# A gated expert layer and feed-forward block: every engine's order of instructions written in the kernel

## Chip, core and metric

The kernel runs on one core of one Trainium2 chip. The metric is the device time of one execution in microseconds (us), as the median of several runs.

## What is computed

There are 2048 tokens with 512 features in float32. A token id chooses one of four experts; the expert's one 512 x 512 matrix serves as gate, up and down projection. The result goes back onto the token, gated by a tanh. Then a layer norm and a feed-forward block follow; its outputs, weighted by the two best of eight routing scores, are summed into the first eight rows of the output.

```
hs = layernorm(x)
g = silu(hs @ M[e].T); u = hs @ M[e].T          # M = ctx_2048, e = expert of the token
x = x + tanh(g_xattn) * ((g * u) @ M[e].T)
xr = layernorm(x)
p = softmax(xr @ wr.T); top 2 of 8 -> gates (normed), indices
h = silu(silu(xr @ w1.T) @ w3.T) @ w2.T
out = zeros; out[indices[:, k]] += gates[:, k] * h   (k = 0, 1)
x = x + tanh(g_ffn) * out
```

## The kernel before

**Passes.** The tokens are sorted by expert into 17 passes of 128 places. Passes 0 to 12 (`NF` = 13) hold one expert each. Passes 13 to 16 are split in four groups of 32 places, each group with its own expert, and so need four matrices. The preamble works out the sorting on VectorE (DVE) with a few small products on TensorE (PE): `from_row` (where the tokens of a pass lie), `to_row` (where they go) and `which` (which expert's matrix a place needs). `which0` is the first pass's entry of that table, worked out ahead of the rest.

**One pass** runs through these steps:
- `gather`: an indirect DMA from POOL's queue brings the pass's rows into one of five buffers x. `load` issues on SP one DMA of 1 MB for a one-expert pass and four for a split pass, into eight buffers m; the row address comes from `which` through a register.
- `prepare`: DVE takes the moments of x and subtracts the mean (`h_a`); PE transposes h_a in four pieces (`tp_a`); ScalarE (ACT) copies the result out of PSUM (`hT`); DVE works out the inverse root of the variance in nine small operations on one column (`rs_a`).
- `up`: PE multiplies by the expert's matrix (`z`), ACT takes a sigmoid with `rs_a` as scale, and DVE multiplies twice (`g`).
- `turn`: PE transposes g (`tp_g`) and ACT copies it (`gT`).
- `down`: PE multiplies again (`y`), DVE adds it onto x, POOL scatters x to the output, and DVE norms the new x (`st_f`, `rs_f`, `h_f`).
- `place_out`: PE transposes h_f (`tp_f`), and ACT copies it into a block's `hT2`. A split pass takes four copies, each to a column read from a table.

**Feed-forward.** Four passes' worth of tokens (512) make a block; there are four blocks. `ffn` is a generator that is advanced by `step()`: four pieces of `u` (w1) with sigmoid and product, one piece for the routing scores (`lg`) and `route`, and four pieces of `v` (w3). At a block's end `acc` adds the four pieces with the gates; the last block takes its last two in turned form (`accT`). After the last block w2 is applied once to the eight sums.

**Order.** The main loop runs over 17 passes and two more iterations. Iteration i issues up(i), place_out(i-2), a step, down(i-1), turn(i), the gather and loads of pass i+3, a step and prepare(i+2). The program text is not the order in which an engine runs it: the tile framework's scheduler orders each engine's instructions itself, by priority and by what it expects to be ready. A few `issue_after` blocks hold instructions behind a named one. The order of passes is a list in the kernel.

```
order = [0, 1, 2, 3, 4, NF, 5, 6, NF + 1, 7, 8, 9, NF + 2, 10, 11, 12, NF + 3]
```

PSUM has four buffers for z, y, u and v (`ps_mm`), three for transposes and lg (`ps_tp`) and one for the sums.

Of the kernel before, what the change touches and what calls it, by code (L numbers as in the profile page):

```python
# [8 lines left out]
F32 = mybir.dt.float32  # L9
# [15 lines left out]
def tile_gated_moe_ffn(  # L25
# [234 lines left out]

    start = ct_([P, 2 * E - 1], F32, "start")
    nc.vector.scalar_tensor_tensor(start, cut[:, 1 : 2 * E], 0.0, steps, ALU.is_le, ALU.mult)
    which0 = ct_([P, 1], I32, "which0")
    with nc.allow_low_precision("whole numbers below 4096"):
        nc.vector.tensor_reduce(which0, start, AX.X, ALU.add)
    from_row = ct_([P, NP], I32, "from_row")
    known = nc.vector.tensor_scalar(from_row, tok, -1.0, 0.0, ALU.add, ALU.max)

    which = ct_([P, NU], I32, "which")
    first = ct_([P, NU - NF], I32, "first")  # L270
    to_row = ct_([P, NP], I32, "to_row")

    later = ct_([P, 2 * E, NU], F32, "later")

    def matrix_table():

        nc.vector.tensor_tensor(
            later,
            place0.unsqueeze(1).to_broadcast([P, 2 * E, NU]),
            cut[:, 1 : 2 * E + 1].unsqueeze(2).to_broadcast([P, 2 * E, NU]),  # L280
            ALU.is_ge,
        )
        stepped = ct_([P, 2 * E - 1, NU], F32, "stepped")
        nc.vector.tensor_tensor(
            stepped,
            later[:, 0 : 2 * E - 1],
            steps.unsqueeze(2).to_broadcast([P, 2 * E - 1, NU]),
            ALU.mult,
        )
        with nc.allow_low_precision("whole numbers below 4096"):  # L290
            nc.vector.tensor_reduce(which, stepped.rearrange("p e n -> p n e"), AX.X, ALU.add)

# [27 lines left out]
    nc.gpsimd.memset(aT, 0.0)  # L320

    def moments(xt, name):
        st = small.tile([P, 6], F32, tag="st", name=f"st_{name}")
        nc.vector.bn_stats(st, xt)  # L324
        mv = small.tile([P, 2], F32, tag="mv", name=f"mv_{name}")
        nc.vector.bn_aggr(mv, st)
        return mv

    def inverse_root(mv, name):


        v = small.tile([P, 1], F32, tag="v", name=f"v_{name}")
        nc.vector.tensor_scalar_add(v, mv[:, 1:2], EPS)  # L333
        r = small.tile([P, 1], F32, tag="r", name=f"r_{name}")
        nc.vector.tensor_scalar(
            r.bitcast(I32), v.bitcast(I32), -0.5, float(0x5F3759DF), ALU.mult, ALU.add
        )
        q = small.tile([P, 1], F32, tag="q", name=f"q_{name}")
        nc.vector.scalar_tensor_tensor(q, r, v, r, ALU.mult, ALU.mult)
        w = small.tile([P, 1], F32, tag="w", name=f"w_{name}")  # L340
        nc.vector.tensor_scalar(w, q, 0.375, -1.25, ALU.mult, ALU.add)
        nc.vector.tensor_scalar(w, w, q, 1.875, ALU.mult, ALU.add)
        nc.vector.tensor_mul(r, r, w)
        nc.vector.scalar_tensor_tensor(q, r, v, r, ALU.mult, ALU.mult)
        nc.vector.tensor_scalar(q, q, -0.5, 1.5, ALU.mult, ALU.add)
        rs = small.tile([P, 1], F32, tag="rs", name=f"rs_{name}")
        nc.vector.tensor_mul(rs, r, q)
        return rs
# [7 lines left out]

    order = [0, 1, 2, 3, 4, NF, 5, 6, NF + 1, 7, 8, 9, NF + 2, 10, 11, 12, NF + 3]
    assert sorted(order) == list(range(NP))
    xs, rss, hTs, gTs, gs, hs2, mats = {}, {}, {}, {}, {}, {}, {}

# [9 lines left out]

    def prepare(p):

        mv = moments(xs[p], f"a{p}")
        h = work.tile([P, D], F32, tag="h", name=f"h_a{p}")
        centred = nc.vector.tensor_scalar(h, xs[p], mv[:, 0:1], None, ALU.subtract)
        tp = transposed(h, f"a{p}")
        hT = work.tile([P, KC * P], F32, tag="hT", name=f"hT_{p}")
        parts = 2 if p == order[0] else 1
        n = KC * P // parts
        for i in range(parts):  # L380
            nc.scalar.copy(hT[:, i * n : (i + 1) * n], tp[:, i * n : (i + 1) * n])  # L381
        hTs[p] = hT
        rss[p] = inverse_root(mv, f"a{p}")
        return centred

    def load(p):
# [3 lines left out]
        for i in range(n0, n0 + n):  # L390
            at = nc.values_load(
                which0[0:1, :] if p == order[0] else which[0:1, i : i + 1],
                engines=[SP],
                min_val=0,
                max_val=(E - 1) * D,
                skip_runtime_bounds_check_because="an expert's number, times D",
            )
            m = mp.tile([P, KC, D], F32, tag="m", name=f"m_{i}")
            dma = nc.sync.dma_start(
                m, ctxT[bass.ds(at, D), :].rearrange("(k p) f -> p k f", p=P)  # L400
            )
            mats[p].append(m)
        return dma

# [22 lines left out]

    def turn(p):
        tp = transposed(gs.pop(p), f"g{p}")
# [4 lines left out]
    def down(p):  # L434
# [12 lines left out]
        )  # L447
        mv = moments(xt, f"f{p}")
        rs = inverse_root(mv, f"f{p}")
        h = work.tile([P, D], F32, tag="h", name=f"h_f{p}")  # L450
        nc.vector.tensor_scalar(h, xt, mv[:, 0:1], rs, ALU.subtract, ALU.mult)  # L451
        hs2[p] = h

    def place_out(p):

# [66 lines left out]
    def ffn(b):  # L522
# [30 lines left out]
        def gated(t):  # L553
# [10 lines left out]
            nc.scalar.activation(s2, v, AF.Sigmoid)  # L564
            return s2, nc.vector.tensor_mul(s2, s2, v)  # L565

# [21 lines left out]
        for t in range(TT):  # L588
            s2, done = gated(t)
            s2s.append(s2)  # L590
            if t < TT - 1:
                yield
            if b == NB - 1 and t == TT - 2:
                for i in range(TT - 2):
                    add(i, s2s[i])
                a = work.tile([P, D], F32, tag="a", bufs=1, name="a")
                nc.scalar.copy(a, acc)
        if b < NB - 1:
            for t in range(TT):
                add(t, s2s[t])  # L600
        else:
            add_turned(TT - 2, s2s[TT - 2])
            tp = transposed(a, "sum")
            with tc.issue_after(done.ins):
                nc.vector.tensor_reduce(
                    aT[:, :, 0:NR],
                    tp.rearrange("p (k t q) -> p k q t", k=KC, t=TT)[:, :, 0:NR, :],
                    AX.X,
                    ALU.add,
                )  # L610
            add_turned(TT - 1, s2s[TT - 1])
        yield


    block_of = [min(p // TT, NB - 1) for p in order]
    ready = {}
    for b in range(NB):
        ready.setdefault(max(i for i in range(NP) if block_of[i] == b), []).append(b)
    AHEAD = 3
    load(order[0])  # L620
    for p in order[:AHEAD]:
        gather(p)
    with tc.issue_after(known.ins):
        matrix_table()
        for p in order[1:AHEAD]:
            load(p)
    centred = prepare(order[0])
    with tc.issue_after(centred.ins):
        prepare(order[1])
        row_tables()  # L630
    running = []

    def step():
        if running and next(running[0], 0) == 0:
            running.pop(0)

    for i in range(NP + 2):
        if i < NP:
            up(order[i])
        if i >= 2:  # L640
            place_out(order[i - 2])
            running += [ffn(b) for b in ready.get(i - 2, [])]
        step()
        if 1 <= i <= NP:
            down(order[i - 1])
        if i < NP:
            turn(order[i])
        if i + AHEAD < NP:
            gather(order[i + AHEAD])
            loaded = load(order[i + AHEAD])  # L650
            with tc.issue_after(loaded.ins):
                if i == 0:
                    w1 = load_w(w1T, "w1")
                    wr = load_w(wrT, "wr")
                if order[i + AHEAD] == NF:
                    w3 = load_w(w3T, "w3")
                    w2 = load_w(w2T, "w2")
        step()
        if i + 2 < NP:
            prepare(order[i + 2])  # L660
    while running:
        step()

    x_first = ct_([P, P], F32, "x_first")
    nc.vector.memset(x_first, 0.0)
    for k in range(KC):
# [55 lines left out]
```

## Time and profile before

| | |
|---|---|
| median of 3 runs | 304.76 us (304.38 to 304.84) |
| profiled execution, its own time | 305.67 us |
| its span in the profile | 303.9 us |
| PE busy | 278.0 us, 91% |
| DVE busy | 153.9 us, 51% |
| ACT busy | 65.6 us, 22% |
| POOL busy | 38.3 us, 13% |
| bytes moved by DMA | 42.54 MB, mean 140 GB/s |

Busy times are unions over an engine's instructions. A float32 matmul appears as two records of 0.592 us each that overlap, so a record's length is not its price; the distance from start to start is. A name such as `z<-m,hT` gives the tile that an instruction writes and those it reads. What ended an idle time is inferred from semaphores. The span is what the profiler saw; the profiled execution's own time has 1.8 us around it.

### The profile page before, as it was taken

The numbers are of one execution on the slowest core, as the hardware profiler recorded it, in microseconds if no ns is written. First come the engines' busy times: TensorE is split into PE (matmuls) and PEld (weight loads), VectorE is DVE, ScalarE is ACT, GpSimd is POOL, SyncE is SP. The second block draws the span as 40 slices with busy tenths as digits, with TensorE's granted clock in tenths as the row PEclk, the third lists the DMA queues.
The fourth block names the chain that finished last, engine by engine and source line by source line (L and its number), as shares of the span: only waits on it lengthen the run. The fifth ranks groups of instructions, "written<-read, shape, count | busy, mean of one in ns | idle before, by whom it ended". The sixth has DMA issues, their size and how long they took to land.

```text
span 303.9 us, 3486 instructions
## 1 busy us (share of the span) xinstructions
PE 278.0 (91%) x1150; PEld 126.4 (42%) x1150; DVE 153.9 (51%) x610; ACT 65.6 (22%) x125; POOL 38.3 (13%) x60
## 2 busy tenths in 40 slices
PE   0169999979999999999799999999989999999994
PEld 0134455524435434535343444445334444344433
DVE  5445477772636954618816276646262455201511
ACT  1012232231312231303302222323021212102120
POOL 5410111311200211101212011100010010000000
PEclk9999999999999999999999999999999999999999
DMA  0799997551509931509925141910000000000000
GB/s 1 230 398 365 409 377 302 208 207 44 179 29 352 345 128 27 181 2 333 405 84 175 36 173 47 372 64 35 0 37 0 35 11 3 0 0 1 2 0 2
DMA packets 20722, 42.54 MB, mean 140 GB/s; under 512 B 2143, under 2 KB 2207, under 8 KB 20704
## 3 DMA queue, kind: packets, MB, share of 16 engines
q1 hardware_dynamic: 17664, 33.66, 30.8%
q0 software_dynamic: 2720, 8.65, 7.8%
q8 instruction: 9, 0.15, 0.2%
q14 instruction: 9, 0.07, 0.1%
q10 hardware_dynamic: 320, 0.01, 0.1%
HBM read 38.10 MB, written 4.47 MB: 140 GB/s over the span
## 4 chain that ended last, share of the span: by engine, by line
PE 85%; DVE 6%; DMA 2%; issue 2%; POOL 2%; ACT 1%; POOLq 0%; ACTq 0%
PE y L410 20%; PE u L529 19%; PE v L556 18%; PE z L410 17%; DMA x<-in_x_dram,from_row 2%; PE tp_a L354 2%; PE tp_f L354 2%; PE tp_g L354 2%; PE acc L568 2%; PE lg L544 1%; DVE x L439 1%; DVE st_f L324 1%; POOL lane L141 1%; DVE st_a L324 1%; DVE h_f L451 0%
## 5 line engine op out<-in xcount | busy, mean ns | idle before, releaser
L410 PE MATMUL z<-m,hT 128*32 128x512 f32 (+1 forms) x232 | 68.0, 612 | 0.5 <-ACT hT L381 0.5
L410 PE MATMUL y<-m,gT 128*32 128x512 f32 (+1 forms) x232 | 64.0, 595 | 0.4 <-ACT gT L431 0.4
L529 PE MATMUL u<-hT,w 128*128 128x512 f32 x128 | 57.9, 597 | 1.5 <-ACT hT L461 1.5
L556 PE MATMUL v<-w,s 128*128 128x512 f32 x128 | 57.2, 595 | 0.0
L410 PEld LDWEIGHTS y<-m,gT 128*32 128x32 f32 (+1 forms) x232 | 23.7, 146 | 33.2 <-issue 31.2
L410 PEld LDWEIGHTS z<-m,hT 128*32 128x32 f32 (+1 forms) x232 | 23.9, 151 | 30.6 <-issue 29.2
L529 PEld LDWEIGHTS u<-hT,w 128*128 128x128 f32 x128 | 23.2, 190 | 28.6 <-issue 25.6
L556 PEld LDWEIGHTS v<-w,s 128*128 128x128 f32 x128 | 23.4, 190 | 26.6 <-issue 25.4
L440 POOL DMA_INDIRECT out_dram<-x,to_row x17 | 17.0, 997 | 116.7 <-DVE x L439 115.8
L439 DVE SCALAR_TENSOR_TENSOR x<-y,tg,x 128x512 f32<-128x512 f32 x17 | 12.8, 751 | 36.0 <-PE y L410 36.0
L538 DVE TENSOR_TENSOR s<-sg,u 128x512 f32<-128x512 f32 x16 | 11.0, 685 | 35.0 <-ACT sg L537 34.9
L424 DVE SCALAR_TENSOR_TENSOR g<-z,rs_a,g 128x512 f32<-128x512 f32 x17 | 12.7, 748 | 29.4 <-ACT g L423 29.4
L363 POOL DMA_INDIRECT x<-in_x_dram,from_row x17 | 16.6, 976 | 72.4 <-issue 27.5
L565 DVE TENSOR_TENSOR s<-s,v 128x512 f32<-128x512 f32 x16 | 11.0, 685 | 27.4 <-ACT s L564 27.4
L537 ACT ACTIVATE sg<-u 128x512 f32<-128x512 f32 x16 | 9.6, 597 | 53.4 <-PE u L529 44.0
L354 PE MATMUL tp_a<-ident,h_a 128*128 128x128 f32 x68 | 11.4, 294 | 10.2 <-DVE v_a L333 5.8
L423 ACT ACTIVATE g<-z,rs_a 128x512 f32<-128x512 f32 x17 | 11.7, 687 | 37.2 <-PE z L410 25.7
L431 ACT COPY gT<-tp_g 128x512 f32<-128x512 f32 x17 | 10.0, 585 | 45.0 <-PE tp_g L354 45.0
L564 ACT ACTIVATE s<-v 128x512 f32<-128x512 f32 x16 | 9.6, 597 | 39.9 <-PE v L556 39.9
L381 ACT COPY hT<-tp_a 128x512 f32<-128x512 f32 (+1 forms) x18 | 10.0, 563 | 37.4 <-PE tp_a L354 37.4
L354 PEld LDWEIGHTS tp_a<-ident,h_a 128*128 128x128 f32 x68 | 8.5, 149 | 20.8 <-issue 15.9
L324 DVE BATCH_NORM_STATS2 st_a<-x 128x6 f32<-128x512 f32 x17 | 11.6, 679 | 6.4 <-DMA x<-in_x_dram,from_row 6.4
(133 smaller groups left out, 209.1 us busy)
## 6 DMA issues: line engine op xcount, KB each, us to landing
m<-in_ctxT_dram SPq DMA_DIRECT2D x29, 1024.0 KB
w<-in_w1T_dram SPq DMA_DIRECT2D x1, 1024.0 KB
w<-in_w3T_dram SPq DMA_DIRECT2D x1, 1024.0 KB
w<-in_w2T_dram SPq DMA_DIRECT2D x1, 1024.0 KB
x<-in_x_dram,from_row POOLq DMA_INDIRECT x17, 4.9
out_dram<-x,to_row POOLq DMA_INDIRECT x17, 4.9
wr<-in_wrT_dram SPq DMA_DIRECT2D x1, 64.0 KB
x_first<-out_dram SPq DMA_DIRECT2D x4, 4.0 KB
```

Of the source, the lines that this page charges most:

```text
L324: nc.vector.bn_stats(st, xt)
L354: nc.tensor.transpose(tp[:, k * P : (k + 1) * P], h[:, k * P : (k + 1) * P], ident)
L363: nc.gpsimd.indirect_dma_start(out=xt, out_offset=None, in_=x, in_offset=bass.IndirectOffsetOnAxis(ap=from_row[:, p : p + 1], axis=0),)
L410: nc.tensor.matmul(out_ps[i * n : (i + 1) * n, :], lhs[:, k * P + i * n : k * P + (i + 1) * n], m[:, k, :], start=(k == 0), stop=(k == KC ...
L423: nc.scalar.activation(g, z, AF.Sigmoid, scale=rs)
L424: nc.vector.scalar_tensor_tensor(g, z, rs, g, ALU.mult, ALU.mult)
L439: nc.vector.scalar_tensor_tensor(xt, y, tg[:, 0:1], xt, ALU.mult, ALU.add)
L440: nc.gpsimd.indirect_dma_start(out=out, out_offset=bass.IndirectOffsetOnAxis(ap=to_row[:, p : p + 1], axis=0), in_=xt, in_offset=None, bou ...
L529: nc.tensor.matmul(u, w1[:, k, m * P : (m + 1) * P], hT[:, k, 0:TB], start=(k == 0), stop=(k == KC - 1),)
L538: nc.vector.tensor_mul(s1[:, m, :], sg, u)
L556: nc.tensor.matmul(v, s1[:, k, t * P : (t + 1) * P], w3[:, k, :], start=(k == 0), stop=(k == KC - 1),)
L565: return s2, nc.vector.tensor_mul(s2, s2, v)
```

## The change

The kernel is traced under `tc.manual_schedule()`: every engine runs its instructions in the order of the program text. The `issue_after` blocks go. The text is arranged anew:

- Each iteration issues up(i), gather and loads of pass i+3, down(i-1), turn_out(i-2), norms, a step, turn_mid(i), turn_in(i+1), a step. `prepare` is cut in two: the norm (`centre` and `scale` ahead of the loop, `norms` in it) and the transposes with their copy (`turn_in`, one pass ahead).
- `norms` works out the second norm of pass i-1 and the first of pass i+2 together; `inverse_roots` alternates the operations of both.
- The first passes are written out ahead of the loop.
- `matrix_table` is called for the first two places ahead of `from_row` and for the rest later; `which0` goes.
- The order of passes changes: split passes come later. The norms' h tiles have four buffers instead of three.
- At a block's end, `acc` is issued with the next step's work (`SHORT`).
- `x_first` is cleared early on POOL, not late in the text on DVE.

The core of the diff:

```diff
-    start = ct_([P, 2 * E - 1], F32, "start")
-    nc.vector.scalar_tensor_tensor(start, cut[:, 1 : 2 * E], 0.0, steps, ALU.is_le, ALU.mult)
-    which0 = ct_([P, 1], I32, "which0")
-    with nc.allow_low_precision("whole numbers below 4096"):
-        nc.vector.tensor_reduce(which0, start, AX.X, ALU.add)
+    def matrix_table(n0, n1):
+        n = n1 - n0
...
+    matrix_table(0, 2)
     from_row = ct_([P, NP], I32, "from_row")
-    known = nc.vector.tensor_scalar(from_row, tok, -1.0, 0.0, ALU.add, ALU.max)
+    nc.vector.tensor_scalar(from_row, tok, -1.0, 0.0, ALU.add, ALU.max)
...
+    x_first = ct_([P, P], F32, "x_first")
+    nc.gpsimd.memset(x_first, 0.0)
...
-    def inverse_root(mv, name):
+    def inverse_roots(mvs_, names):
+        n = range(len(names))
...
+        for i in n:
+            nc.vector.tensor_scalar_add(v[i], mvs_[i][:, 1:2], EPS)
+        for i in n:
+            nc.vector.tensor_scalar(
+                r[i].bitcast(I32), v[i].bitcast(I32), -0.5, float(0x5F3759DF), ALU.mult, ALU.add
+            )
...
-    order = [0, 1, 2, 3, 4, NF, 5, 6, NF + 1, 7, 8, 9, NF + 2, 10, 11, 12, NF + 3]
+    order = [0, 1, 2, 3, 4, 5, 6, NF, 7, 8, NF + 1, 9, 10, NF + 2, 11, 12, NF + 3]
...
+    def centre(p):
+        mvs[p] = moments(xs[p], f"a{p}")
+        hs[p] = work.tile([P, D], F32, tag="h", bufs=4, name=f"h_a{p}")
+        nc.vector.tensor_scalar(hs[p], xs[p], mvs[p][:, 0:1], None, ALU.subtract)
+    def scale(*ps):
+        for p, rs in zip(ps, inverse_roots([mvs.pop(p) for p in ps], [f"a{p}" for p in ps])):
+            rss[p] = rs
+    def turn_in(p):
+        tp = transposed(hs.pop(p), f"a{p}")
...
+    def norms(p_in, p_out):
+        names, mv = [], []
+        if p_out is not None:
+            xt = x1s.pop(p_out)
+            mv.append(moments(xt, f"f{p_out}"))
+            names.append(f"f{p_out}")
+        if p_in is not None:
+            mv.append(moments(xs[p_in], f"a{p_in}"))
+            names.append(f"a{p_in}")
+        rs = inverse_roots(mv, names)
...
         if b < NB - 1:
             for t in range(TT):
                 add(t, s2s[t])
+            yield SHORT
...
+    def step():
+        if running:
+            r = next(running[0], 0)
+            if r == 0:
+                running.pop(0)
+            if r in (0, SHORT):
+                step()
     load(order[0])
+    load(order[1])
+    for i in range(5):
+        gather(order[i])
+    centre(order[0])
+    turn_in(order[0])
+    centre(order[1])
+    scale(order[0], order[1])
+    matrix_table(2, NU)
+    load(order[2])
+    w1 = load_w(w1T, "w1")
+    wr = load_w(wrT, "wr")
+    load(order[3])
+    row_tables()
+    centre(order[2])
+    scale(order[2])
+    up(order[0])
+    turn_in(order[1])
+    up(order[1])
+    turn_mid(order[0])
+    turn_in(order[2])
+    down(order[0])
+    turn_mid(order[1])
+    norms(order[3], order[0])
+    load(order[4])
+    w3 = load_w(w3T, "w3")
+    w2 = load_w(w2T, "w2")
-    for i in range(NP + 2):
+    for i in range(2, NP + 2):
         if i < NP:
             up(order[i])
-        if i >= 2:
-            place_out(order[i - 2])
-            running += [ffn(b) for b in ready.get(i - 2, [])]
+        if i + 3 < NP:
+            gather(order[i + 3])
+            load(order[i + 3])
+        if i <= NP:
+            down(order[i - 1])
+        else:
+            step()
+        turn_out(order[i - 2])
+        if i <= NP:
+            norms(order[i + 2] if i + 2 < NP else None, order[i - 1])
         step()
-        if 1 <= i <= NP:
-            down(order[i - 1])
+        running += [ffn(b) for b in range(NB) if last[b] == i - 2]
         if i < NP:
-            turn(order[i])
...
+            turn_mid(order[i])
+        if i + 1 < NP:
+            turn_in(order[i + 1])
         step()
-        if i + 2 < NP:
-            prepare(order[i + 2])
     while running:
         step()
...
-    with tile.TileContext(nc) as tc:
+    with tile.TileContext(nc) as tc, tc.manual_schedule():
         tile_gated_moe_ffn(tc, *args)
```

More of the change, by code (lines that the diff above doesn't have):

```diff
@@ L259, in tile_gated_moe_ffn @@
         )
-    start = ct_([P, 2 * E - 1], F32, "start")
-    nc.vector.scalar_tensor_tensor(start, cut[:, 1 : 2 * E], 0.0, steps, ALU.is_le, ALU.mult)
-    which0 = ct_([P, 1], I32, "which0")
-    with nc.allow_low_precision("whole numbers below 4096"):
-        nc.vector.tensor_reduce(which0, start, AX.X, ALU.add)
-    from_row = ct_([P, NP], I32, "from_row")
-    known = nc.vector.tensor_scalar(from_row, tok, -1.0, 0.0, ALU.add, ALU.max)
     which = ct_([P, NU], I32, "which")
-    first = ct_([P, NU - NF], I32, "first")
-    to_row = ct_([P, NP], I32, "to_row")
     later = ct_([P, 2 * E, NU], F32, "later")
-    def matrix_table():
+    stepped = ct_([P, 2 * E - 1, NU], F32, "stepped")
+    def matrix_table(n0, n1):
+        n = n1 - n0
         nc.vector.tensor_tensor(
-            later,
-            place0.unsqueeze(1).to_broadcast([P, 2 * E, NU]),
-            cut[:, 1 : 2 * E + 1].unsqueeze(2).to_broadcast([P, 2 * E, NU]),
+            later[:, :, n0:n1],
+            place0[:, n0:n1].unsqueeze(1).to_broadcast([P, 2 * E, n]),
+            cut[:, 1 : 2 * E + 1].unsqueeze(2).to_broadcast([P, 2 * E, n]),
             ALU.is_ge,
         )
-        stepped = ct_([P, 2 * E - 1, NU], F32, "stepped")
         nc.vector.tensor_tensor(
-            stepped,
-            later[:, 0 : 2 * E - 1],
-            steps.unsqueeze(2).to_broadcast([P, 2 * E - 1, NU]),
+            stepped[:, :, n0:n1],
+            later[:, 0 : 2 * E - 1, n0:n1],
+            steps.unsqueeze(2).to_broadcast([P, 2 * E - 1, n]),
             ALU.mult,
@@ L290, in matrix_table @@
         with nc.allow_low_precision("whole numbers below 4096"):
-            nc.vector.tensor_reduce(which, stepped.rearrange("p e n -> p n e"), AX.X, ALU.add)
+            nc.vector.tensor_reduce(
+                which[:, n0:n1], stepped[:, :, n0:n1].rearrange("p e n -> p n e"), AX.X, ALU.add
+            )
+    matrix_table(0, 2)
+    from_row = ct_([P, NP], I32, "from_row")
+    nc.vector.tensor_scalar(from_row, tok, -1.0, 0.0, ALU.add, ALU.max)
+    first = ct_([P, NU - NF], I32, "first")
+    to_row = ct_([P, NP], I32, "to_row")
     def row_tables():
@@ L327, in moments, with new @@
         return mv
-    def inverse_root(mv, name):
[L332 to L347, printed above, removed]
+    def inverse_roots(mvs_, names):
+        n = range(len(names))
+        def new(tag):
+            return [small.tile([P, 1], F32, tag=tag, name=f"{tag}_{name}") for name in names]
+        v, r, q, w, rs = new("v"), new("r"), new("q"), new("w"), new("rs")
+        for i in n:
[3 more added lines that the diff above has]
+                r[i].bitcast(I32), v[i].bitcast(I32), -0.5, float(0x5F3759DF), ALU.mult, ALU.add
+            )
+        for i in n:
+            nc.vector.scalar_tensor_tensor(q[i], r[i], v[i], r[i], ALU.mult, ALU.mult)
+        for i in n:
+            nc.vector.tensor_scalar(w[i], q[i], 0.375, -1.25, ALU.mult, ALU.add)
+        for i in n:
+            nc.vector.tensor_scalar(w[i], w[i], q[i], 1.875, ALU.mult, ALU.add)
+        for i in n:
+            nc.vector.tensor_mul(r[i], r[i], w[i])
+        for i in n:
+            nc.vector.scalar_tensor_tensor(q[i], r[i], v[i], r[i], ALU.mult, ALU.mult)
+        for i in n:
+            nc.vector.tensor_scalar(q[i], q[i], -0.5, 1.5, ALU.mult, ALU.add)
+        for i in n:
+            nc.vector.tensor_mul(rs[i], r[i], q[i])
         return rs
@@ L355, in transposed @@
         return tp
-    order = [0, 1, 2, 3, 4, NF, 5, 6, NF + 1, 7, 8, 9, NF + 2, 10, 11, 12, NF + 3]
+    order = [0, 1, 2, 3, 4, 5, 6, NF, 7, 8, NF + 1, 9, 10, NF + 2, 11, 12, NF + 3]
     assert sorted(order) == list(range(NP))
-    xs, rss, hTs, gTs, gs, hs2, mats = {}, {}, {}, {}, {}, {}, {}
+    xs, x1s, mvs, rss, hs, hTs, gTs, gs, hs2, mats = {}, {}, {}, {}, {}, {}, {}, {}, {}, {}
     def gather(p):
@@ L369, in gather @@
         xs[p] = xt
[L371 to L376, printed above, removed]
+    def centre(p):
[7 more added lines that the diff above has]
+        tp = transposed(hs.pop(p), f"a{p}")
         hT = work.tile([P, KC * P], F32, tag="hT", name=f"hT_{p}")
@@ L382, in prepare @@
         hTs[p] = hT
-        rss[p] = inverse_root(mv, f"a{p}")
-        return centred
     def load(p):
@@ L391, in load @@
             at = nc.values_load(
-                which0[0:1, :] if p == order[0] else which[0:1, i : i + 1],
+                which[0:1, i : i + 1],
                 engines=[SP],
@@ L398, in load @@
             m = mp.tile([P, KC, D], F32, tag="m", name=f"m_{i}")
-            dma = nc.sync.dma_start(
-                m, ctxT[bass.ds(at, D), :].rearrange("(k p) f -> p k f", p=P)
-            )
+            nc.sync.dma_start(m, ctxT[bass.ds(at, D), :].rearrange("(k p) f -> p k f", p=P))
             mats[p].append(m)
-        return dma
     def expert_product(out_ps, lhs, p):
@@ L426, in up, with turn_mid @@
         gs[p] = g
-    def turn(p):
+    def turn_mid(p):
         tp = transposed(gs.pop(p), f"g{p}")
@@ L447, in down, with turn_out @@
         )
[L448 to L454, printed above, removed]
+        x1s[p] = xt
+    def norms(p_in, p_out):
[8 more added lines that the diff above has]
+        rs = inverse_roots(mv, names)
+        if p_out is not None:
+            h = work.tile([P, D], F32, tag="h", bufs=4, name=f"h_f{p_out}")
+            nc.vector.tensor_scalar(h, xt, mv[0][:, 0:1], rs[0], ALU.subtract, ALU.mult)
+            hs2[p_out] = h
+        if p_in is not None:
+            rss[p_in] = rs[-1]
+            hs[p_in] = work.tile([P, D], F32, tag="h", bufs=4, name=f"h_a{p_in}")
+            nc.vector.tensor_scalar(hs[p_in], xs[p_in], mv[-1][:, 0:1], None, ALU.subtract)
+    def turn_out(p):
         tp = transposed(hs2.pop(p), f"f{p}").rearrange("p (k t) -> p k t", k=KC)
@@ L564, in gated @@
             nc.scalar.activation(s2, v, AF.Sigmoid)
-            return s2, nc.vector.tensor_mul(s2, s2, v)
+            nc.vector.tensor_mul(s2, s2, v)
+            return s2
         def add(t, s2):
@@ L588, in ffn @@
         for t in range(TT):
[L589 to L592, printed above, removed]
+            s2s.append(gated(t))
             if b == NB - 1 and t == TT - 2:
@@ L597, in ffn @@
                 nc.scalar.copy(a, acc)
+            yield
         if b < NB - 1:
@@ L603, in ffn @@
             tp = transposed(a, "sum")
[L604 to L610, printed above, removed]
-            add_turned(TT - 1, s2s[TT - 1])
[L612 to L630, printed above, removed]
+            nc.vector.tensor_reduce(
+                aT[:, :, 0:NR],
+                tp.rearrange("p (k t q) -> p k q t", k=KC, t=TT)[:, :, 0:NR, :],
+                AX.X,
+                ALU.add,
+            )
@@ L631, in tile_gated_moe_ffn @@
+            add_turned(TT - 1, s2s[TT - 1])
+    SHORT = 1
+    last = {b: max(i for i, p in enumerate(order) if min(p // TT, NB - 1) == b) for b in range(NB)}
     running = []
     def step():
-        if running and next(running[0], 0) == 0:
-            running.pop(0)
-    for i in range(NP + 2):
+        if running:
[4 more added lines that the diff above has]
+                step()
+    load(order[0])
+    load(order[1])
@@ L643, in tile_gated_moe_ffn @@
         step()
-        if 1 <= i <= NP:
-            down(order[i - 1])
+        running += [ffn(b) for b in range(NB) if last[b] == i - 2]
         if i < NP:
-            turn(order[i])
[L648 to L657, printed above, removed]
+            turn_mid(order[i])
@@ L658, in tile_gated_moe_ffn @@
+        if i + 1 < NP:
+            turn_in(order[i + 1])
         step()
-        if i + 2 < NP:
-            prepare(order[i + 2])
     while running:
         step()
-    x_first = ct_([P, P], F32, "x_first")
-    nc.vector.memset(x_first, 0.0)
     for k in range(KC):
```

## The prediction

> **What bounds the kernel now.** I read the page first, for the engine that carries the time.
>
> ```profile
> PE 278.0 (91%) x1150; PEld 126.4 (42%) x1150; DVE 153.9 (51%) x610; ACT 65.6 (22%) x125; POOL 38.3 (13%) x60
> ...
> PE 85%; DVE 6%; DMA 2%; issue 2%; POOL 2%; ACT 1%; POOLq 0%; ACTq 0%
> ```
>
> TensorE is busy for 91% of the span and is 85% of the chain that ended last. The change removes no matmul, so only the stretches in which PE waits or works badly can be won. I looked for them in PE's own timeline. Its columns are start, duration, instruction, count, and in brackets the idle time before it and what ended that.
>
> ```profile
> 17.35 2.07 PE L410 MATMUL z<-m,hT 128*128 128x512 f32 x2 [0.46 <-ACT hT L381]
> ...
> 36.08 3.60 PE L410 MATMUL z<-m,hT 128*128 128x512 f32 x8
> ...
> 60.72 3.64 PE L410 MATMUL z<-m,hT 128*32 128x512 f32 x32
> 65.59 0.63 PE L354 MATMUL tp_a<-ident,h_a 128*128 128x128 f32 x4 [1.23 <-DVE h_a L375]
> 66.05 0.60 PE L354 MATMUL tp_f<-ident,h_f 128*128 128x128 f32 x4
> 67.43 3.70 PE L529 MATMUL u<-hT,w 128*128 128x512 f32 x8 [0.78 <-ACT hT L461]
> ...
> 106.53 1.90 PE L410 MATMUL z<-m,hT 128*32 128x512 f32 x10
> 108.42 0.63 PE L354 MATMUL tp_a<-ident,h_a 128*128 128x128 f32 x4
> 108.98 2.77 PE L410 MATMUL z<-m,hT 128*32 128x512 f32 x22
> ...
> 215.20 1.06 PE L568 MATMUL acc<-s,g 128*32 128x512 f32 x6
> 216.19 1.13 PE L410 MATMUL y<-m,gT 128*128 128x512 f32 x2
> 217.24 1.04 PE L568 MATMUL acc<-s,g 128*32 128x512 f32 x2
> ```
>
> The reader sees three kinds of loss: PE idle at the start of a feed-forward block (60 to 67 us), a four-expert product cut in two by a transpose (106 us), and the fourth `acc` product set apart from its three fellows (217 us). Start-to-start times give the clean prices: an uninterrupted product (z, y, u or v) 3.44, four transposes 0.44, lg 1.01, four `acc` products together 0.99. A four-expert product costs 0.15 more, and so do the transposes behind it.
>
> I split PE at the first z of the third pass (36.08) and at the end of v of block 2 (264.29). Between these lie 15 z, 16 y, 12 u and 12 v (55 x 3.44 = 189.2), 46 sets of transposes (20.1), 3 lg (3.0), 2 `acc` (2.0) and 8 four-expert extras (2.3): 216.6. The interval is 228.2, so **11.6 us** are lost in it. By place: 2.6 at 60-67, 2.5 at 145-152, 1.6 at 221-227, 1.3 and 1.4 at two late `acc`, 1.0 twice at cut z, 0.5 in small pieces: 11.9, the same within rounding.
>
> [...] a scatter whose input was done on DVE at 44.8 us starts at 45.90, behind the gather of 44.62. [...] 32 records of 0.592 us finish in 3.64. [...] The first z records stand 0.85 apart until 27.2 us, then 0.43. [...] Here the gather of x, issued before the matrices pile up, lands in 3.5 us; the next, issued with two of them, in 7.6.
>
> **Part by part.**
>
> *Table of matrices in two pieces, loads moved on SP.* `which0` (0.16 + 0.15 on DVE) goes; `matrix_table(0, 2)` adds three small operations (about 0.6), under the tok matmuls (1.11 on PE). Its result comes with `from_row`, near 9.7, not at 6.7. The first matrix then leaves SP at about 10.4 instead of 7.38 and, by its old pace (all bytes moved 4.6 us later), lands at 15.0. The first z needs `hT` at 18.5 (below): hidden by 3.5 us. The third matrix, w1, wr and the fourth wait for the rest of the table, which now stands behind the norms of two passes, near 23.6; at 1 MB in 2.6 us and 4.6 for the first, the fourth lands by about 37. Its z starts near 44: hidden. The later loads are asked for three passes ahead into 8 buffers. The tightest is the last four-expert set: two of its matrices need buffers freed at the y one and a half iterations earlier, 17 us, and need 4.6 + 2.6: hidden. If that cover failed, PE would wait for each microsecond missing.
>
> *The first x.* Its gather issues at about 10.4 as before (10.52), but now beside the first two matrices. Landing: 13.9 if nothing is lost, 17.3 if it takes nearly what the second took. I take 15.3, the first matrix's landing plus a little, and keep both ends.
>
> *Start of PE.* Centring takes 1.6 (14.07 to 15.66), cold transposes and half copy 1.55: z0 at 18.5. Before, z0 was cut after two records while PE waited for the second x (19.53). Now it runs through: six cold records and two warm, 5.1 + 0.9, end 24.5. Then transposes, with the copy of hT behind the sigmoid on ACT (0.69 + 0.58 + handoffs): z1 starts 1.5 later, 26.0; 3.70 after a wait; sigmoid and copy of gT 1.4, y0 at 31.1 to 34.8, transposes 0.44. On DVE, x1 at 18.4, its centring, 18 root steps at 0.13, two tables (1.3 + 1.4), the third pass's norm (3.1) and g (1.5) end at 29.7, just as z1 does. With 0.2 for that tie z2 starts at **35.4 instead of 36.08: -0.7** (34.0 to 37.4 by the landing).
>
> *The loop.* Each iteration issues z(i), y(i-1), transposes of f(i-2), a step, transposes of g(i) and a(i+1), a step. f's chain starts at y and has the rest of an iteration, a z and a y (8.2 us) against 5.8 on DVE (x 0.76, two moments 1.7, 18 root steps 2.3, two h 1.0): hidden. g's chain, 2.4 after z, lies under y: hidden. The copy of hT(i+1) lies under the second step, even when that is lg (1.01). At the start of blocks 0 and 1 the copy of f lies under two transposes (0.88 against 0.7). DVE per iteration with two steps is 8.7 of 15 us. So the 11.6 us go. Side by side roots bring nothing of their own: before, r_f and r_a already alternate at 0.13.
>
> *What comes back.* Where no step follows, z(i+1) waits for ACT: three copies 0.48 apart (31.48, 31.94), the last 0.58, against 0.88 of transposes, 0.8, and 0.27 for restart (3.70 for 3.43). That is 1.1 before each of the fourth, fifth and sixth z, and 1.1 before the last, where four copies of a split pass (1.55) stand in front but `acc` covers 0.99. Block 2 starts under one set of transposes only: 0.5. Behind lg 0.3. Sum **5.2**; bounds 3.5 (waits without restarts) and 7.5 (a second ACT hand-off at each). Net -6.4. In the tail all four `acc` of block 2 stand behind the last v; the fourth waits 1.45 for sigmoid and product, then takes 0.98: 2.43 against 2.16 before, **+0.3**.
>
> *No cost.* The memset of `x_first` moves from DVE to POOL, which is idle from 5 to 10 us. The new pass order moves block 1 one pass earlier; PE does the same work. POOL issues gather(i+3) ahead of scatter(i-1); the gather waits for scatter(i-2) to free one of five x buffers (6.9 us, below), and the scatter behind it has an iteration of slack.
>
> **Sum:** -0.7 - 6.4 + 0.3 = -6.8. The profiled execution took 305.67 (span 303.9) and would take 298.9; the shown median, 304.76, is 0.9 below it, so **298.0**.
>
> **Rivals.**
>
> *Late first x* (0.24). The same, but x lands at 17.3, behind both matrices, as the 7.6 of the second says it may; for the milder case speaks that the second matrix issues after the first gather starts. +2.0: 300.0.
>
> *Slower: the x ring* (0.11). gather(i+3) is tied to scatter(i-2), and its moments stand on DVE ahead of everything later.
>
> ```profile
> POOL x L363 <- DMA out_dram<-x,to_row: 25.7, 4, 6.9
> ```
>
> From y(i-2): 0.9 to the scatter, 7.7 to its landing, 7.6 at most for the gather: 16.2. The short iterations allow 2 x 9.3 + 1.5 = 20.1. If the traffic of ten matrices stretches the trip beyond that, DVE stops with g and x behind it and PE loses the excess in up to three iterations. It decides from (6.8 / 3) = 2.3 beyond, a trip of 22.4; at 23.0 the loss is 8.7: 306.7. Against it speaks the 4 us of slack.
>
> *The order is not what the change says* (0.05): if the engines' orders stayed much as they are, the time is 304.8.
>
> **How the numbers follow.** The forecast has 0.60. Its own range is x's landing (-1.4, +2.0) with the returned waits (-1.7, +2.3), not all at once: 295.5 to 300.5. With the late start the range is **295.0 to 301.5**. About 0.2% is what a measurement of this kernel can tell from no change. Faster: 0.60 + 0.24 = 0.84; same: most of the unchanged order, 0.04; slower: 0.11 + 0.01 = 0.12.
>
> **What would show it.** Right: no four-expert z cut by transposes; four `acc` together at blocks 0 and 1; waits of PE on "ACT hT L381" of about 0.8, a handful; third z near 35; almost no waits on DVE h. Wrong: idle PE ahead of tp_f or tp_g (DVE late), moments waiting on x for microseconds within the loop, PE waiting for m, or transposes still inside products.

## Result, and the profile after

The changed kernel takes **299.26 us** (median of 4 runs, 299.16 to 299.39), the kernel before 304.8 beside it: ratio 0.9821, 95% interval 0.9804 to 0.9838. The span falls from 303.9 to 297.4 us. The first two lines are the busy times and the chain that ended last, from the page of the changed kernel.

```profile
PE 271.3 (91%) x1150; PEld 125.8 (42%) x1150; DVE 158.4 (53%) x610; ACT 64.1 (22%) x125; POOL 38.6 (13%) x61
...
PE 88%; ACT 4%; issue 3%; DMA 2%; POOL 1%; DVE 1%; ACTq 0%; POOLq 0%
```

ACT has risen on the chain and DVE has all but gone. PE is at 91% as before, although the span is shorter: of its busy time between the third z and the end of v of block 2, 4.9 us are gone (223.2 before, 218.3 after). A product that is cut in two or runs apart from its fellows counts as busy, so the share of busy time doesn't show such a loss.

The list of PE's waits (total us, times, longest) says where ACT sits. Before, transposes of h_a waited for DVE three times, 4.4 us together (1.8 of it ahead of the third z). In the loop nothing of that is left; the one wait on h_a that remains is that of the very first transposes, 5.8 us before.

```profile
PE tp_a L366 <- DVE h_a L387: 8.2, 1, 8.2
PE z L423 <- ACT hT L399: 4.4, 6, 0.8
PE acc L598 <- DVE s L594: 0.4, 1, 0.4
```

PE's own timeline of the changed kernel (start, duration, instruction, count, idle before it and what ended that):

```profile
19.83 5.42 PE L423 MATMUL z<-m,hT 128*128 128x512 f32 x8 [0.46 <-ACT hT L399]
...
35.44 3.60 PE L423 MATMUL z<-m,hT 128*128 128x512 f32 x8
...
44.56 3.70 PE L423 MATMUL z<-m,hT 128*128 128x512 f32 x8 [0.78 <-ACT hT L399]
...
66.55 3.60 PE L423 MATMUL y<-m,gT 128*128 128x512 f32 x8
...
71.29 3.67 PE L558 MATMUL u<-hT,w 128*128 128x512 f32 x8
...
133.48 3.64 PE L423 MATMUL z<-m,hT 128*32 128x512 f32 x32
...
141.12 1.06 PE L598 MATMUL acc<-s,g 128*32 128x512 f32 x8
...
215.23 3.64 PE L423 MATMUL z<-m,hT 128*32 128x512 f32 x32 [0.73 <-ACT hT L399]
...
257.08 1.06 PE L598 MATMUL acc<-s,g 128*32 128x512 f32 x6
258.56 1.05 PE L598 MATMUL acc<-s,g 128*32 128x512 f32 x2 [0.42 <-DVE s L594]
```

The three losses of before are gone from the middle: a four-expert z runs as one piece (133.48), four `acc` stand together (141.12), and no block starts with idle PE of over a microsecond: block 0 (71.29) starts without a wait. The times say why. Before, y of the block's last pass ended at 60.2 and only one product, z at 60.72, stood between it and the transposes of its f at 66.05, which the norm behind y did not let start earlier. Now a z (63.01) and a y (66.55) stand between. What is new is 0.78 us of idle PE before an ordinary z (44.56, the same before the next two, and 0.73 before the last z, at 215.23).

All kernels below are measured on **three stretches**: S, the start of the third pass's z; V, the start of what follows v of block 2; and the tail from V to the end of the span. Of V − S, 216.6 us is clean work, as the prediction worked out; the rest is lost. (V is taken here at the first `acc`, 264.22 before, 0.07 ahead of the end that the prediction took.)

| | S | lost in V − S | tail | span |
|---|---|---|---|---|
| before | 36.08 | 11.5 | 39.7 | 303.9 |
| after | 35.44 | 5.0 | 40.3 | 297.4 |
| difference | −0.6 | −6.5 | +0.6 | −6.5 |

The loss is the steady one of the three: E5 and E10 below, with the changed kernel's loop, lose 5.0 as well. S is not. Six kernels that have the same text up to it (the changed kernel, E1, E2, E3, E8 and E9) have S between 34.91 and 36.30 in their profiles, so a difference of −0.6 in S proves nothing by itself.

### The profile page after: what moved, and what is told of

The parts are those of the page before. It is cut to its first block, busy times and chain, and to the rows that moved or that the text cites. A ratio compares the mean times of both kernels' runs of the same rounds, so it can differ in the third digit from the quotient of the medians.

```text
span 297.4 us, 3491 instructions
## 1 busy us (share of the span) xinstructions
PE 271.3 (91%) x1150; PEld 125.8 (42%) x1150; DVE 158.4 (53%) x610; ACT 64.1 (22%) x125; POOL 38.6 (13%) x61
## 4 chain that ended last, share of the span: by engine, by line
PE 88%; ACT 4%; issue 3%; DMA 2%; POOL 1%; DVE 1%; ACTq 0%; POOLq 0%
PE z L423 21%; PE y L423 20%; PE v L585 19%; PE u L558 19%; PE tp_f L366 3%; DMA x<-in_x_dram,from_row 2%; PE tp_a L366 2%; PE tp_g L366 2%; PE lg L573 1%; ACT hT L399 1%; PE acc L598 1%; ACT hT L490 1%; ACT gT L444 1%; POOL lane L142 1%; PE o L712 0%
## 5 line engine op out<-in xcount | busy, mean ns | idle before, releaser
L423 PE MATMUL z<-m,hT 128*32 128x512 f32 (+1 forms) x232 | 63.6, 604 | 4.4 <-ACT hT L399 4.4
L423 PE MATMUL y<-m,gT 128*32 128x512 f32 (+1 forms) x232 | 61.8, 596 | 0.4 <-ACT gT L444 0.4
L558 PE MATMUL u<-hT,w 128*128 128x512 f32 x128 | 57.0, 594 | 0.2 <-ACT hT L490 0.2
L423 PEld LDWEIGHTS y<-m,gT 128*32 128x32 f32 (+1 forms) x232 | 23.1, 145 | 36.7 <-issue 36.1
L437 DVE SCALAR_TENSOR_TENSOR g<-z,rs_a,g 128x512 f32<-128x512 f32 x17 | 12.7, 750 | 33.0 <-ACT g L436 33.0
L366 PE MATMUL tp_a<-ident,h_a 128*128 128x128 f32 x68 | 10.7, 282 | 8.2 <-DVE h_a L387 8.2
L490 ACT COPY hT<-tp_f 128x512 f32<-128x512 f32 x13 | 7.6, 586 | 43.3 <-PE tp_f L366 43.3
L438 DVE SCALAR_TENSOR_TENSOR g<-z,rs_a,g 128x512 f32<-128x512 f32 x17 | 12.8, 751 | 0.6
```

The costliest lines, as they stand in the source:

```text
L366: nc.tensor.transpose(tp[:, k * P : (k + 1) * P], h[:, k * P : (k + 1) * P], ident)
L423: nc.tensor.matmul(out_ps[i * n : (i + 1) * n, :], lhs[:, k * P + i * n : k * P + (i + 1) * n], m[:, k, :], start=(k == 0), stop=(k == KC ...
L437: nc.vector.scalar_tensor_tensor(g, z, rs, g, ALU.mult, ALU.mult)
L438: nc.vector.scalar_tensor_tensor(g, z, rs, g, ALU.mult, ALU.mult)
L558: nc.tensor.matmul(u, w1[:, k, m * P : (m + 1) * P], hT[:, k, 0:TB], start=(k == 0), stop=(k == KC - 1),)
```

## Experiments

The kernel before had medians of 304.5 to 305.7 us in these jobs, and its single runs lay between 301.8 and 307.0. So kernels of different jobs are compared by their ratio to it (with its 95% interval) or by the stretches of their profiles, not by their microseconds. E6 and E7 ran twice each, the others 4 to 18 times.

### Undoing the change, one part at a time

**E5: the new text, order left to the scheduler.**

```diff
-    with tile.TileContext(nc) as tc, tc.manual_schedule():
+    with tile.TileContext(nc) as tc:
```

> The changed text, but ordered by the scheduler again (no manual_schedule). Theory: what counts is the order that PE gets; the scheduler keeps the new text's order on PE nearly everywhere behind the start, so about 299.3, plus up to 2 for the start where it puts the whole table of matrices ahead of from_row on DVE and both first transposes ahead of the first z: 299 to 301.5. Rival: the gain comes from taking the ordering away from the scheduler: 303 to 305.

299.82 us, ratio 0.983 (0.9759 to 0.99). S is 36.42, the loss 5.0, the same as with the written order. So the rearranged text carries the gain; that the order is binding brings at most the start (1.0 in S, with PE's first transposes at 20.21 instead of 18.28), which a ratio of this width can't tell from nothing.

**E6: the old text, run as written** (its `issue_after` blocks out, the order binding).

> The text of the kernel before, run in program order (manual_schedule, the issue_after blocks dropped). Theory: writing an order down brings nothing by itself; this text has prepare(i+2) right behind the norm of pass i-1 and its transposes in front of the next z, so PE waits in each iteration for x, two norms and h, about 6.2 after y, of which a step covers 3.4: 2.5 in about nine iterations and 5.5 in about six, some 50 more: 340 to 360. Rival: a fixed order is itself the gain: 300 or less.

390.4 us, ratio 1.28 (1.268 to 1.2923): beyond what either theory gave. The list of waits and two stretches of PE's timeline of E6:

```profile
PE tp_a L354 <- DVE v_a L333: 65.5, 17, 7.9
```
```profile
133.69 0.63 PE L354 MATMUL tp_a<-ident,h_a 128*128 128x128 f32 x4 [2.84 <-DVE v_a L333]
134.16 5.30 PE L410 MATMUL z<-m,hT 128*128 128x512 f32 x8
...
192.75 1.09 PE L354 MATMUL tp_a<-ident,h_a 128*128 128x128 f32 x4 [5.12 <-DVE v_a L333]
193.63 4.70 PE L410 MATMUL z<-m,hT 128*128 128x512 f32 x8
```

PE stalls for 65.5 us, 7.9 of it for the first x, and behind a stall it works slowly: after 5.12 us transposes take 1.09 instead of 0.6 and a z 4.70 instead of 3.6; after 2.84 us a z takes 5.30. All z together are busy for 85.8 us, 22.2 more than in the changed kernel (63.6), which the expectation left out. The mean granted clock, the share of PE's full clock that the profile shows, is 0.915. The scheduler had been hiding the old text's order; binding it needs another text.

**E7: no pipelining by one.** f of pass i−1 is transposed in the iteration of its own y, behind the first step, and blocks start an iteration earlier; all else as changed. (Pipelining by one is no part of the change: the kernel before has it too.)

```diff
-        turn_out(order[i - 2])
...
+        turn_out(order[i - 1])
```

> The changed kernel, but turn_out of pass i-1 is issued in iteration i behind the first step, not an iteration later; blocks are added an iteration earlier. Theory: the pipelining by one carries the loop. Now PE waits for the chain behind y (5.4 to h_f): 2.3 in some ten iterations with a step, about 5 in some five without: 30 to 50 more, 330 to 350. Rival: the chain is hidden by other work, since DVE is busy for 53% only: within 2 of 299.3.

364.27 us, ratio 1.1945 (1.1834 to 1.2056). PE's waits and its timeline in E7:

```profile
PE tp_f L366 <- DVE h_f L476: 46.7, 17, 5.0
```
```profile
70.35 1.09 PE L366 MATMUL tp_f<-ident,h_f 128*128 128x128 f32 x4 [5.04 <-DVE h_f L476]
...
73.82 5.87 PE L423 MATMUL z<-m,hT 128*128 128x512 f32 x8 [0.68 <-ACT hT L399]
```

The second norm's 5.0 us lie bare in an iteration without a step, and z then takes 5.87. That it is the order that holds PE shows in what stands behind: g for the next transposes was done on DVE before 65 (its two operations are all that DVE worked on from 55 to 65, 1.50 us), and they start at 71.23, behind those of f. With a step between y and the transposes of f the wait is still 1.5 to 1.6 in most iterations. The span is 65.2 longer than the changed kernel's, of which the waits on `h_f` are 46.7; the rest is mostly slow work behind them (PE is busy for 288.6 us instead of 271.3), which the expectation left out. Pipelining by one is what makes a binding order bearable.

**E2: `acc` straight behind the fourth v** at every block's end.

> The changed kernel, but the four acc products of a block are issued right behind its fourth v, not with the next step's work. Theory: the fourth acc product then waits 1.45 for sigmoid and product and stands alone, 2.46 as block 2 shows it, not 0.99, at blocks 0 and 1: +2.9 in all, about 302.2. Block 2 is unchanged. Rival: PE has slack behind them (next z waits for hT anyway), so +0 to +0.5: 299.3 to 299.8.

303.47 us, ratio 0.9926 (0.9904 to 0.9949); the loss is 8.9, 3.9 more than after. The late `acc` cost 1.47 at block 1 (207.22 to 209.68, against 0.99) and about 1.3 at block 0, close to what was expected. The third microsecond shows in PE's timeline of E2: no `acc` stands over the copies ahead of the last z, which waits 1.81 instead of 0.73.

```profile
217.52 0.60 PE L366 MATMUL tp_a<-ident,h_a 128*128 128x128 f32 x4
219.93 3.64 PE L423 MATMUL z<-m,hT 128*32 128x512 f32 x32 [1.81 <-ACT hT L399]
```

**E3: transposes put back into the four-expert z** (`turn_in(i+1)` behind the fifth of its 16 products).

> The changed kernel, but in iterations whose z is a four-expert product the transposes of turn_in stand inside it, behind the fifth of its 16 matmuls, as the scheduler had put them in the kernel before. Theory: a cut costs 1.0 (1.05 and 1.02 before), three cuts: +3.1, about 302.4. Rival: the cut's price before was a wait that happened to stand there[...]: 299.3, within 0.5.

302.83 us, ratio 0.9933 (0.9902 to 0.9965); the loss is 8.4, +3.4 for three cuts. PE's timeline of E3:

```profile
89.80 1.90 PE L425 MATMUL z<-m,hT 128*32 128x512 f32 x10
91.63 0.66 PE L366 MATMUL tp_a<-ident,h_a 128*128 128x128 f32 x4
92.22 2.77 PE L425 MATMUL z<-m,hT 128*32 128x512 f32 x22
```

From 89.80 to 94.92 pass 5.12 us, where an uncut z (3.57) and transposes (0.44 to 0.53) take 4.0 to 4.1. So one cut costs about 1.05.

**E4: the two inverse roots one after the other** on DVE.

> The changed kernel, but the nine operations of one inverse root come before the nine of the other, instead of alternating. Theory: each dependent operation costs about 0.2 instead of 0.13, so a pair takes some 1.2 longer on DVE, off the chain that sets the end: 299.3, within 0.4. Rival: DVE's norms set the pace (side-by-side roots are what the gain rests on): 1.2 in each of 14 iterations, up to 316.

300.58 us, ratio 0.9852 (0.9797 to 0.9907): more than the theory's 0.4, far from the rival's 316. DVE needs 3.6 us for the 18 small operations where it took 2.0 alternating. PE's timeline of E4 shows where this comes through:

```profile
31.15 0.66 PE L358 MATMUL tp_g<-ident,g 128*128 128x128 f32 x4 [0.91 <-DVE g L430]
...
44.67 0.63 PE L358 MATMUL tp_g<-ident,g 128*128 128x128 f32 x4 [0.75 <-DVE g L430]
```

Only at the start and in the first iteration of the loop, where g stands behind the roots in DVE's queue: S is 1.0 later and the loss 0.9 larger. This 1.0 is no chance of the first z, for z1 starts at the same time in both (26.54 and 26.51). In the later iterations, with a step or without, no transposes of g wait for DVE: in the next one g is done at 52.7 and its transposes come at 53.87.

**E8: the old order of passes** in the new text.

> The changed kernel with the order of passes of the kernel before. Theory: block 1 is ready a pass later, so an iteration without a second step comes at z of the twelfth pass instead of the last: one wait of 1.05 comes and one goes, 299.3, within 0.6. Rival: the pass order is part of the gain, because four matrices are wanted earlier (sixth pass) and PE waits for m: 301 or more.

298.87 us, ratio 0.9804 (0.9733 to 0.9876), loss 4.6: the order of passes brings nothing that can be told from none.

### What came back: the copy of hT

**E1: transposes of the next h_a straight behind z**, ahead of y.

```diff
             up(order[i])
+        if i + 1 < NP:
+            turn_in(order[i + 1])
...
-        if i + 1 < NP:
-            turn_in(order[i + 1])
```

> The changed kernel with one move: turn_in(order[i+1]) is issued between up(i) and down(i-1), not behind turn_mid(i). Theory of the ledger: the five waits of PE on the copy of hT (four in the loop, 0.78 + 0.78 + 0.78 + 0.73 with 0.27 of restart each) go under y, and nothing else moves: 4 x 1.05 = 4.2 off 299.3, about 295.1; the 0.24 at the start of block 2 stays. Rival: ACT, in order, is what sets these stretches (DVE or ACT late next), and z then waits for g or x: less than half of it, 297 to 299.

300.92 us, ratio 0.9865 (0.981 to 0.992); loss 7.1. Both theories missed. The waits on hT in the loop vanish, but PE's timeline of E1 shows another in their place, with y behind it:

```profile
40.07 0.63 PE L366 MATMUL tp_a<-ident,h_a 128*128 128x128 f32 x4 [1.56 <-DVE h_a L481]
```

h_a(i+1) is made in the same `norms` as h_f(i−1) and is done about 5.3 us after y(i−1) ended (39.93 against 34.63); z ends 3.9 after it here and 4.3 in the next iterations, where the wait is 1.1. One product is too little cover. This led to E9, with two.

**E9: transposes of the next h_a between y and those of f** (behind those of f where a block starts).

```diff
+        starts = any(last[b] == i - 2 for b in range(NB))
+        if i + 1 < NP and not starts:
+            turn_in(order[i + 1])
         turn_out(order[i - 2])
+        if i + 1 < NP and starts:
+            turn_in(order[i + 1])
...
-        if i + 1 < NP:
-            turn_in(order[i + 1])
```

> The transposes of h_a for the next pass stand between y and the transposes of f in every iteration (behind those of f where a block starts), all else as in the changed kernel. Theory: the waits of about 1.05 us ahead of the fourth, fifth, sixth and last z are the copy of hT on ACT, and vanish if the copy has the transposes of f and g (0.88) beside it; at this place h_a is done (it is made beside z and y, 9 us after the last y, where the transposes straight behind z came 4.8 after it and waited for it). The rest lost between the third pass's z and v of block 2 falls from 5.0 to about 0.8; about 295.1 us, ratio 0.968. Rival: as with the transposes straight behind z, another wait takes the place (h_a on DVE, or the copy of hT2 on ACT): 297 or more, with idle PE ahead of tp_a, tp_f or u.

295.56 us, ratio 0.9709 (0.9643 to 0.9775). PE's timeline of E9:

```profile
42.56 0.60 PE L366 MATMUL tp_a<-ident,h_a 128*128 128x128 f32 x4
43.00 0.60 PE L366 MATMUL tp_f<-ident,h_f 128*128 128x128 f32 x4
43.44 0.60 PE L366 MATMUL tp_g<-ident,g 128*128 128x128 f32 x4
43.90 3.70 PE L423 MATMUL z<-m,hT 128*128 128x512 f32 x8
```

z follows its transposes at once, so two products are enough. The loss is 1.5: 3.5 less than after, of the 4.2 expected. What is left is the start of block 2 (0.6) and about 0.1 in many places, which had been counted into the price of a wait.

### The first x

Three lines of the changed kernel: the loads on SP's queue, the first gather on POOL, and the first moments on DVE, each from its engine's timeline.

```profile
10.55 0.43 SPq L415 DMA_DIRECT2D m<-in_ctxT_dram  x1
```
```profile
10.57 1.13 POOL L375 DMA_INDIRECT x<-in_x_dram,from_row  x1 [5.54 <-DVE from_row L287]
```
```profile
16.71 0.69 DVE L326 BATCH_NORM_STATS2 st_a<-x 128x6 f32<-128x512 f32 x1 [6.43 <-DMA x<-in_x_dram,from_row]
```

x lands 6.1 us after its issue, beside two matrices (the second issues at 11.47); before, it was 3.5.

**E10: the separate first table entry is back**, and the first matrix leaves at 7.26.

> The separate first entry of the matrix table is put back, so that the first matrix leaves SP near 7.4 us, 3 us ahead of the first gather, as before; all else as in the changed kernel. Theory: the first x landed at 16.7 because both matrices moved beside it (6.1 us where the kernel before shows 3.5); now the first has mostly moved when the gather starts, x lands near 14.5 and the third pass's z starts 1 to 2 us earlier[...]: 297.8 to 298.6. Rival: the second matrix alone, issued with the gather, holds it back as much: x lands near 16.5, 299.2 or a little more for two added operations on DVE.

298.82 us, ratio 0.9815 (0.9748 to 0.9881). The theory missed. In E10 the second matrix leaves SP at 10.66, ahead of the gather, and x is there at 16.43, 5.5 after its issue:

```profile
10.89 1.13 POOL L380 DMA_INDIRECT x<-in_x_dram,from_row  x1 [5.86 <-DVE from_row L292]
```
```profile
16.43 0.69 DVE L331 BATCH_NORM_STATS2 st_a<-x 128x6 f32<-128x512 f32 x1 [5.83 <-DMA x<-in_x_dram,from_row]
```

The rival had it: one matrix asked for just ahead of the gather held it nearly as long as two (5.5 us against 6.1).

### Putting it together

**E11: E9 and E10, a rearranged start, and `acc` of block 2 behind the first u of block 3.** At the start the transposes of the second h_a go inside the first z, those of g inside the second.

> Together: transposes of h_a between y and those of f, the first matrix's own table entry, at the start the transposes of the second pass inside the first z and those of g inside the second z (the third pass's norm behind them), and acc of block 2 behind the first u of block 3 instead of in the tail. Theory: the lost time between the third z and v of block 2 falls from 5.0 to about 0.8 (-4.2), the third z starts 1.5 to 3 earlier, the late fourth acc of block 2 is covered (-1.4): 290.5 to 292.5, ratio 0.953 to 0.96. Rival: the pieces meet the same limit, DVE's norms ahead of h_a and g in the start: z of the third pass no earlier than 34.5 and waits on DVE in the first iterations: 294 to 296.

293.12 us, ratio 0.9629 (0.9577 to 0.968). This is a little outside what the theory gave (290.5 to 292.5). S is 34.74, the loss 1.6, the tail 38.7. The loss fell by 3.5 of the 4.2 expected. The tail fell by 1.6, about 1.4 of it at `acc`, as expected; PE's timeline of E11 shows the late `acc` covered:

```profile
252.91 3.60 PE L568 MATMUL u<-hT,w 128*128 128x512 f32 x8
256.44 1.07 PE L610 MATMUL acc<-s,g 128*32 128x512 f32 x8
```

All four now take 1.00 instead of 2.46. The start gave 0.7 of the 1.5 to 3 expected, no more than S varies by anyway, for x came at 16.53, as in E10.

**E12: E11 with the second matrix later.** Its table entries stand behind `from_row` and the first part of the rest of the table; `matrix_terms` and `matrix_sums` are the two halves of `matrix_table`.

```diff
-    matrix_table(0, 2)
     from_row = ct_([P, NP], I32, "from_row")
     nc.vector.tensor_scalar(from_row, tok, -1.0, 0.0, ALU.add, ALU.max)
+    matrix_terms(2, NU)
+    matrix_terms(0, 2)
+    matrix_sums(0, 2)
```

> The combined kernel again (e11), with one thing moved: the table entries for the second matrix stand behind from_row and behind the first part of the rest of the table on DVE, so that the second matrix leaves SP about 1.4 us later than in e11 (near 12.1 instead of 10.65) and the first gather about 0.4 earlier; only the first matrix is then under way when that gather starts. Theory: what held the first x at 16.5 (5.6 us after its issue at 10.88) was the second matrix, asked for 0.2 us ahead of it; x lands 3.5 to 4 us after its issue, near 14.2, as before the change, and the third pass's z starts 1.3 to 2 us earlier than 34.74; about 291.4 us. Rival: the first matrix, still moving until about 11.5, and the gathers behind it hold x as much: x lands at 16 or later, and the time stays within 0.6 us of 293.1.

**291.17 us, ratio 0.9544 (0.9513 to 0.9575)**, the fastest. Three lines of E12, from the timelines of SP, POOL and DVE:

```profile
12.36 0.39 SPq L424 DMA_DIRECT2D m<-in_ctxT_dram  x1
```
```profile
10.96 1.13 POOL L384 DMA_INDIRECT x<-in_x_dram,from_row  x1 [5.94 <-DVE later L273]
```
```profile
14.54 0.69 DVE L335 BATCH_NORM_STATS2 st_a<-x 128x6 f32<-128x512 f32 x1 [2.68 <-DMA x<-in_x_dram,from_row]
```

With the second matrix 1.4 us behind the gather, x lands 3.6 us after its issue and S is 32.60. The gather itself was not earlier, against the expectation; `from_row` waits for PE's tok. Against the changed kernel, E12's span is 8.0 shorter: 2.8 in S, 3.5 in the loss, 1.7 in the tail. Here S lies 2.3 below the lowest of the six kernels with the changed kernel's start, and the first x lands 2.2 earlier than in the changed kernel.

## Why the prediction was right, and where it was off

Forecast 298.0, range 295.0 to 301.5; measured 299.26, faster by 1.8%. The three terms of the sum, −0.7, −6.4 and +0.3, measured −0.6, −6.5 and +0.6. The mechanism of the middle term, which is nearly all of the gain, held. That all three agree so well is in part luck, as the start and the tail show. And the order need not have been binding: the scheduler, given the new text, keeps the same 5.0 (E5).

- **Start (35.4 forecast, 35.44 measured): right by two errors that cancel.** The first x was put at 15.3 and landed at 16.7, nearer to the rival "late first x" (17.3), so that z0 began at 19.83 instead of 18.5. It was won back. z0 to z1 took 6.7 instead of 7.5, for four records of z0 were slow (0.85 apart until 23.38, then 0.43), not six, as many as were slow from 22.11 to 27.2 in the kernel before. The profile shows a granted clock of 1.00 in both stretches, so why they are slow was not shown. Four instead of six is chance, since the same z0 took from 4.74 to 6.10 in other profiles. z1 to z2 took 8.9 instead of 9.4: the prediction priced z1 and y0 at 3.70, the length of a product's records, but from start to start they take 3.54 (z1, 26.51 to 30.05), and no tie with DVE showed. The landing was argued from the first matrix; E10 and E12 show what decided here: whether any matrix, the first or the second, is asked for at the time of the gather (5.5 us to the landing in E10, 6.1 in the changed kernel). One that was asked for 3.6 us earlier did not hold it up (E12: 7.33 and 10.96, x there after 3.6).
- **The 11.6 lost.** Each kind went where the order said it would. Put back singly, a cut z costs 1.05 (E3: 3.4 for three) and a late `acc` 1.47 (E2). E7 shows that the norm of f, which the prediction called hidden with 8.2 us of cover for 5.8, is hidden only by the pipelining: without it 46.7 us of waits. The largest kind, the start of the blocks (2.6, 2.5 and 1.6 by the prediction's count), was not put back by a run of its own. That a second product between y and the transposes of f removed it is read from the two timelines; nearest to a test are the waits of 1.5 to 1.6 in E7 with one product between.
- **The 5.2 that come back.** Measured 5.0: four waits of 0.9 to 1.05 (forecast 1.1), 0.6 at block 2 (0.5), the rest in small pieces. E9 removes the four and shows them to be the copy of hT. The 0.27 that the prediction adds for a restart compares the length of the records, 3.70, with a price from start to start, 3.43. From start to start the z at 44.56 takes 3.54, so the restart is 0.10; the gap ahead of it, from 43.62 where the transposes would have been done, is 0.94, not 0.8. The two errors nearly cancel.
- **Side by side roots "bring nothing of their own".** Against the kernel before that holds, since its roots already alternated. As part of the new order they are worth about 1.6 (E4: spans of 299.0 and 297.4), at the start, where the prediction had counted DVE's queue to end "just as z1 does" with a tie of 0.2.
- **Tail (+0.3 forecast, +0.6 measured).** `acc` is +0.3 as worked out. The other 0.35 is the last product, 1.43 instead of 1.08, with a granted clock of 0.68 (292.4 to 294) instead of 1.00. The prediction had no such term, and it is no effect of the change: with the same end of the text the last product took 1.08 in E1, E4 and E5 and 1.65 in E3.
- **The x ring** did not become the bound: in the loop no moments waited for x; the only two waits of moments on x, 7.0 us together, are at the start.
- **The step that was mis-sized** is the last: 298.9 in the profiled execution was close (299.16), but 0.9 was then taken off to forecast the median, because the profiled execution of before lay 0.9 above its median. The changed kernel's profiled execution lies 0.1 below its own. An offset of one execution is not a property of the kernel and does not carry over to the next.

That the written order binds PE, on which the prediction leaned, E7 shows: transposes whose g was done before 65 start at 71.23, behind late ones. What a matrix costs the gather, E10 and E12 measure only as a whole: 5.5 and 3.6 us from issue to landing. How the transfers share their way was not shown, and why a matrix asked for 0.2 us ahead delays the gather by 2 us was not settled.

## What to carry to other kernels

When you write an engine's order by hand, ask for each instruction how much work stands between it and what it waits for, on every engine: one product (3.4 us) was too little for a norm and two were enough (E1 and E9), and moving four transposes by two places was worth 3.5 us. Of a chain of copies that ends in the operand of the next product, put the copy that is needed first at the head. When a small load is what everything waits for, hold the large ones back until it is under way: 1.4 us were enough here (E12). And when work is busy but badly placed, look at the distance from start to start, for the busy share stays where it was.

## What the runs showed of the hardware that was not expected

- **In E6 and E7 a stall cost more than its length.** In E7, 5.04 us of idle PE were followed by transposes at 1.09 and a z of 5.87 instead of 3.6; the mean granted clock was 0.65 from 65 to 75, 0.84 from 75 to 85 and 1.00 from 95 to 105. Over the whole span it was 0.947 in E7 and 0.915 in E6, against 0.993 in the changed kernel. In E6 shorter stalls did it too: idle times of 2.84 us ahead of the transposes at 113.63, 133.69 and 171.53 were followed by a z of 5.13, 5.30 and 5.25. Behind a wait of 1.81 us in E2 z still took 3.64, and behind waits of 1.6 in E7 (106.70, 138.17) u and v took 3.60.
- **The first z varies by over a microsecond** between profiles of kernels with the same start: 4.74 us in E1, 5.42 in the changed kernel, 6.10 in E2. The spread of S, 34.91 to 36.30, comes from it: from E1 to E2 z0 grows by 1.36 and S by 1.39. That is of the size of the smaller effects here, and a reason to read S and the loss apart.
